# Start addresses of the large tiles in a two-layer graph network: three fill tiles

## The chip, the cores and the metric

The kernel runs on one core of a Trainium2 chip. The metric is the device time of one execution in microseconds; the number before is the median of three runs. A profiled execution supplies the trace that the views below are taken from. PE is the tensor engine, DVE the vector engine, ACT the scalar engine, POOL is GpSimd, and SP issues most of the loads.

## The reference

`x` is 8 batches of 2,048 nodes with 64 features (fp32), `adj` a 2,048 x 2,048 matrix in which the nonzero values of a row are all 1 / (their number). Two layers, each with a layer norm over `x + layer(x)`:

```python
# layer 0: per-node weights from an embedding of 16 numbers
w = einsum('nd,dkio->nkio', embedding, weight)
b = einsum('nd,do->no', embedding, bias)
As = [I, adj, 2 * adj @ adj - I]
x_g = einsum('knm,bmc->bnkc', stack(As), x)
x = layernorm(x + einsum('bnki,nkio->bno', x_g, w) + b)
# layer 1: [x, A x, 2 A A x - x] twice (both supports are adj), then one projection
x = layernorm(x + concat(x0, A x0, 2 A A x0 - x0, A x0, 2 A A x0 - x0) @ W1 + b1)
```

## The kernel before

The product of `adj` with node features is called a hop. There are four of them (two for each layer), each over 16 blocks of 128 source nodes. For each block a slab of `adj` is loaded into a tile `raw` (lines 170 to 175, or 506 in the last stage), and DVE turns it into a tile `s` of ones and zeros in fp32r (`places` at L179, `places_equal` at L185, `places_counted` at L192). The features of the block are split into two fp32r halves in a tile `hl` of 4,096 bytes in each partition: a rounded copy by ACT (L198) and the remainder by DVE (L199). PE then multiplies, 16 matmuls with 512 columns of the moving operand for each slab of 1,024 nodes. The degree of the node is multiplied in as the sums leave PSUM.

The stages follow one another on PE:

- `hop_x` (first hop, two halves of the target nodes): `add_block`, L206. `s` gives the weights, a half of `hl` is the moving operand. 512 matmuls.
- `hop_z1` (second hop): L388, the other way round. `hl` gives the weights, and `s` is the moving operand. 512 matmuls.
- the mixing with per-node weights, one tile of 128 nodes after another: L314 in `mix0`, plain fp32, 64 rows in each of two row groups, 256 columns; weights from `xt`, `t1` and `z2`, the moving operand is `w`. DVE sums up at L320, and `project` (L333) prepares the second layer.
- the third hop, `hop_h`, in pieces of 4, 8 and 4 target tiles: L206 again, 512 matmuls.
- the fourth hop, first `hop_g` for eight target tiles at once, then `hop_tile` for the others one by one: L206, 512 matmuls, with the `hl` tiles of all 16 blocks kept in the pool `flate`. Layer norm and stores are done beside the matmuls.

`run` (L211) calls the operands of a step two steps ahead of its matmuls. Loads go through SP in program order. `raw` has 6 buffers, `s` has 4, and `hl` has 3 until the fourth hop.

Where the tiles lie: pools take memory from the left or, with `side="right"`, from the right end, one behind the other; each tile is rounded up to 32 bytes in the partition. A tile lies at the same place in all partitions. On the left, 16,384 bytes for descriptors and four constants of 32 bytes each come first, then `flag` (L819) and the pools in the order of lines 63 to 75, `flate` taking the place of `fconst` and `fwork2` later. In the program before, the tiles start as follows (bytes in the partition, and the remainder by 128):

```
flag   16512   0      acc   82784  96      rrow   143584  96
z1     16544  32      eT/xc 94432  96      w0     157408  96
z2     49312  32      raw  102624  96      xt     170720  96
rcol   82080  32      s    127200  96      t1     175392  32
equal  82144  96      hl   143584  96 (flate, fourth hop)
sums   82528  96      z0   184288  96      hl     217056  96 (right)
```

Further buffers of a tile follow at multiples of its size. Rows of `hl` and slices of `s` that a matmul takes start 512 bytes, or a multiple of that, behind the start of their tile.

The lines that the change touches are those of the pools on the right (L70 to L72), the tiles of `keep` (L93 to L98, with `sums` at L485) and `flag`.

Of the kernel before, what the change touches and what calls it, by code (L numbers as in the profile page):

```python
# [8 lines left out]
F32 = mybir.dt.float32  # L9
F32R = mybir.dt.float32r  # L10
I32 = mybir.dt.int32
# [5 lines left out]
P = 128  # L17
# [5 lines left out]
FIRST = 8  # L23
HL = 3
RAW = 6
SLOTS = 3


# [7 lines left out]
def pattern(  # L36
# [23 lines left out]
    def pool(stack, name, bufs, **kw):  # L60
        return stack.enter_context(tc.tile_pool(name=name, bufs=bufs, **kw))

    keep = pool(ctx, "fkeep", 1)
    work = pool(ctx, "fwork", 2)
    xcpool = pool(ctx, "fxc", 4)
    rawp = pool(ctx, "fraw", RAW)
    spool = pool(ctx, "fs", 4)
    psum = pool(ctx, "fps", 4, space=PSUM)

    hops = ctx.enter_context(ExitStack())  # L70
    hpool = pool(hops, "fhl", HL, side="right")
    z0pool = pool(hops, "fz0", 1, side="right")  # L72
    layer0 = ctx.enter_context(ExitStack())
# [22 lines left out]
    nonzero = keep.tile([P, 3 * NT], F32, tag="nonzero", name="nonzero")  # L96
    eps = keep.tile([P, 1], F32, tag="eps", name="eps")
    part = keep.tile([P, B], F32, tag="part", name="part")  # L98
    rrow = const.tile([P, N], F32, tag="rrow", name="rrow")
    ident = const.tile([P, P], F32, tag="ident", name="ident")  # L100
    emb_sb = const.tile([P, NT, D], F32, tag="emb", name="emb_sb")
# [441 lines left out]
def general(  # L543
# [17 lines left out]
    work = ctx.enter_context(tc.tile_pool(name="work", bufs=2))  # L561
    apool = ctx.enter_context(tc.tile_pool(name="adj", bufs=SLOTS))
    ps_hop = ctx.enter_context(tc.tile_pool(name="ps_hop", bufs=2, space=PSUM))
# [59 lines left out]
    def load_block(t, tag):  # L623
        a = apool.tile([P, NT, P], F32, tag="a", name=f"a{t}_{tag}")
        nc.sync.dma_start(out=a, in_=rows(adj, t))
        blocks[t] = a

    def prefetch(o, i, tag):
        if i + SLOTS < NT:
            load_block(o[i + SLOTS], tag)  # L630

    def next_order(o):

        return o[NT - SLOTS :] + o[: NT - SLOTS]

# [119 lines left out]
    with tc.tile_pool(name="slab", bufs=1) as spool:  # L755
        slabs = []
        for k in range(NT):
            nc.scalar.dma_start(out=z[k][:, 0], in_=x[k])
            slabs.append(spool.tile([P, FIRST, P], F32, tag=f"s{k}", name=f"s{k}"))
            nc.sync.dma_start(out=slabs[k], in_=adj[0, k].rearrange("m (t n) -> m t n", n=P))  # L760
        for i in range(SLOTS):
            load_block(FIRST + i, 0)
# [53 lines left out]
def gnn_kernel(tc, x, xT, adj, diag, emb, embT, w0, b0, w1, b1, out):  # L816
    nc = tc.nc
    with tc.tile_pool(name="flag", bufs=1) as fpool:
        flag = fpool.tile([1, 1], I32, tag="flag", name="flag")  # L819
        odd = pattern(tc, x, xT, adj, diag, emb, embT, w0, b0, w1, b1, out, flag)  # L820
        with tc.If(odd > 0):
            general(tc, x, adj, emb, embT, w0, b0, w1, b1, out)
# [39 lines left out]
```

## Time and profile before

| | |
|---|---|
| median of three runs | 861.15 us (861.08 to 861.74) |
| time of the profiled execution | 861.28 us |
| its span, first to last instruction | 859.5 us |
| mean granted clock of PE | 0.995 |
| L206, hops by `add_block`, matmul busy (1,280 + 256) | 293.7 + 58.5 us |
| L388, second hop, matmul busy (512) | 116.3 us |
| L314, mixing, matmul busy (three groups of 1,024, overlapping) | 161.0, 160.0, 159.9 us |
| L320, sums of the mixing on DVE (512) | 246.3 us |

A line of groups gives engine, operation, the tiles written and read, shapes and count, then busy time, the mean ns of one, and the idle time of the engine before them with what ended it. Matmuls are pipelined: the mean of one is its latency, and several are under way at once, so that a pace is to be read from busy time and count or from the starts in the timeline. Each fp32 matmul of the mixing appears as two MATMUL records. [...]

### The profile page before, as it was taken

The page shows a single profiled execution, that of the slowest core. Times are in us where ns is not written, and L with a number is a line of the kernel's source. Part 1 is how long each engine was busy: PE and PEld are TensorE (multiplying, and loading weights), DVE is VectorE, ACT ScalarE, POOL GpSimd, SP SyncE. Part 2 cuts the span into 40 slices and gives each one's busy share as a digit, 9 for nine tenths or more (in the row PEclk, how much of TensorE's full clock was granted, in tenths as well). Part 3 has the DMA queues.
Part 4 walks back from the last instruction along what each step waited for, and adds up shares of the span by engine and source line. Part 5 has one row for each costly group of instructions (what it writes and reads, how often), then busy time and mean ns, then how long its engine had stood idle before and what let it go on. Part 6 is the DMA issues. An engine that isn't in the chain of part 4 may idle for free.

```text
span 859.5 us, 14028 instructions
## 1 busy us (share of the span) xinstructions
PE 834.9 (97%) x5666; PEld 744.9 (87%) x5666; DVE 558.8 (65%) x1146; ACT 162.6 (19%) x311; POOL 118.1 (14%) x125
## 2 busy tenths in 40 slices
PE   7999999999999999999999999999999999999995
PEld 5888888888888999999999999999878888788784
DVE  4336355575467888777787787877866467614562
ACT  2112121121111111111111011111331134201210
POOL 3000000030021222111111111110101020102033
PEclk9999999999999999999999999999999999999998
DMA  9996544444210000000000000000246226641572
GB/s 289 404 220 175 155 133 148 147 144 137 74 37 14 14 13 14 14 13 14 14 13 14 1 14 14 14 13 2 72 156 214 86 85 197 198 146 50 140 215 90
DMA packets 48505, 83.94 MB, mean 98 GB/s; under 512 B 10240, under 2 KB 26624, under 8 KB 48304
## 3 DMA queue, kind: packets, MB, share of 16 engines
q1 hardware_dynamic: 44432, 74.10, 29.0%
q0 software_dynamic: 1408, 4.37, 2.0%
q10 hardware_dynamic: 2592, 4.49, 1.4%
q8 instruction: 47, 0.77, 0.4%
q14 instruction: 26, 0.21, 0.1%
HBM read 78.75 MB, written 4.19 MB: 97 GB/s over the span
## 4 chain that ended last, share of the span: by engine, by line
PE 70%; DVE 17%; issue 7%; POOL 2%; ACT 2%; DMA 1%; DVEq 0%; ACTq 0%; POOLq 0%
PE acc L206 33%; PE pm L314 15%; DVE acc L320 14%; PE accT L388 13%; PE a L206 7%; POOL xc L281 1%; DVE ss L273 1%; ACT sq L272 1%; PE pu L333 1%; POOL xt L414 1%; ACT hl L198 1%; DMA b_sb<-in_b 1%; ACT ln_sd L259 0%; DVE ln_r L261 0%; POOL got L290 0%
## 5 line engine op out<-in xcount | busy, mean ns | idle before, releaser
L206 PE MATMUL acc<-hl,s 128*128 128x512 f32 x1280 | 293.7, 391 | 3.7 <-DVE s L192 2.1
L206 PEld LDWEIGHTS acc<-hl,s 128*128 128x128 f32 x1280 | 240.9, 189 | 55.6 <-issue 3.4
L320 DVE SCALAR_TENSOR_TENSOR acc<-pm,emb_sb,acc 128x256 f32<-128x256 f32 x512 | 246.3, 483 | 47.7 <-PE pm L314 25.1
L314 PE MATMUL pm<-w,xt 64*128 64x256 f32 x1024 | 161.0, 379 | 3.4 <-DVE acc L320 3.4
L314 PE MATMUL pm<-w,t 64*128 64x256 f32 x1024 | 160.0, 376 | 0.2 <-ACT t L242 0.2
L314 PE MATMUL pm<-w,z 64*128 64x256 f32 x1024 | 159.9, 376 | 0.0
L198 ACT CAST hl<-z 128x512 fp32r<-128x512 f32 x128 | 78.1, 622 | 251.9 <-PE acc L206 156.8
L388 PE MATMUL accT<-s,hl 128*128 128x512 f32 x512 | 116.3, 389 | 0.0
L314 PEld LDWEIGHTS pm<-w,xt 64*128 64x128 f32 x1024 | 108.3, 187 | 6.1 <-PE pt L240 3.7
L388 PEld LDWEIGHTS accT<-s,hl 128*128 128x128 f32 x512 | 96.0, 188 | 20.0 <-DVE z L368 0.2
L314 PEld LDWEIGHTS pm<-w,t 64*128 64x128 f32 x1024 | 110.8, 187 | 1.8 <-ACT t L242 0.6
L314 PEld LDWEIGHTS pm<-w,z 64*128 64x128 f32 x1024 | 110.8, 187 | 1.2
L179 DVE TENSOR_SCALAR s<-raw 128x1024 fp32r<-128x1024 f32 x64 | 47.8, 748 | 87.6 <-PE acc L206 77.1
L199 DVE TENSOR_TENSOR hl<-z,hl 128x512 fp32r<-128x512 f32 x128 | 94.5, 746 | 8.1 <-ACT hl L198 8.0
L185 DVE SCALAR_TENSOR_TENSOR s<-raw,rrow 128x1024 fp32r<-128x1024 f32 x32 | 41.3, 1290 | 49.3 <-PE accT L388 43.4
L192 DVE TENSOR_SCALAR_CACHE_REDUCE s<-raw 128x512 fp32r<-128x512 f32 (+1 forms) x48 | 41.2, 860 | 37.5 <-PE acc L206 30.5
L206 PE MATMUL a<-hl,s 128*128 128x512 f32 x256 | 58.5, 389 | 0.9 <-DVE flag L474 0.9
L206 PEld LDWEIGHTS a<-hl,s 128*128 128x128 f32 x256 | 48.0, 188 | 11.0 <-issue 1.0
L414 POOL DMA_DIRECT2D xt<-in_xT x16 | 9.2, 578 | 272.6 <-PE pm L314 201.5
L242 ACT COPY hT<-pt 128x512 f32<-128x512 f32 x16 | 9.4, 586 | 166.5 <-PE pt L240 166.5
L230 POOL TENSOR_TENSOR z<-z,got 128x512 f32<-128x512 f32 x12 | 17.4, 1481 | 160.2 <-ACT got L229 160.1
L340 ACT COPY z<-pu 128x256 f32<-128x256 f32 x64 | 20.7, 375 | 83.5 <-PE pu L333 83.5
(74 smaller groups left out, 339.3 us busy)
## 6 DMA issues: line engine op xcount, KB each, us to landing
raw<-in_adj SPq DMA_DIRECT2D x112, 512.0 KB, 4.3
raw<-in_adj SPq DMA_DIRECT2D x32, 256.0 KB, 2.8
z<-in_x SPq DMA_DIRECT2D x16, 256.0 KB, 8.9
xt<-in_xT POOLq DMA_DIRECT2D x16, 256.0 KB, 2.9
out<-got ACTq DMA_DIRECT2D x16, 256.0 KB, 2.1
w<-in_w SPq DMA_DIRECT2D x6, 256.0 KB, 9.3
rrow<-in_diag SPq DMA_DIRECT2D x1, 1024.0 KB, 8.7
eT<-in_embT ACTq DMA_DIRECT2D x1, 256.0 KB, 3.9
```

Source lines behind the costliest of these rows:

```text
L179: nc.vector.tensor_scalar(s, raw, 0.0, None, ALU.not_equal)
L185: nc.vector.scalar_tensor_tensor(s, raw, 0.0, rrow[:, n0 : n0 + raw.shape[1]], ALU.add, ALU.is_equal, accum_out=count)
L192: nc.vector.tensor_scalar(s, raw, 0.0, 0.0, ALU.not_equal, ALU.add, accum_out=count)
L198: nc.scalar.copy(hl[:, 0], src)
L199: nc.vector.tensor_tensor(hl[:, 1], src, hl[:, 0], ALU.subtract)
L206: nc.tensor.matmul(a, lhsT=s[:, i * P : (i + 1) * P], rhs=hl[:, h], start=(first and h == 0), stop=(last and h == 1),)
L230: nc.gpsimd.tensor_tensor(z[s][t], z[s][t], got, ALU.add)
L314: nc.tensor.matmul(pm[:, j, i], lhsT=tt[k][q, 2 * g + i, :], rhs=w[k][q, ds, :], start=(k == 0), stop=(k == 2),)
L320: nc.vector.scalar_tensor_tensor(part, pm[:, :, :, d, :].rearrange("p j i c -> p (j i) c"), emb_sb[:, t, dd : dd + 1], part, ALU.mult, ALU.add
L340: nc.scalar.copy(bc(s, t)[:, bs, :].rearrange("p (i j) c -> p j i c", j=2), got[:, :, :, 2 - s, :])
L388: nc.tensor.matmul(accs[i][:, c], lhsT=hl[:, h, i * P : (i + 1) * P], rhs=s[:, c * 512 : (c + 1) * 512], start=(k == 0 and h == 0), stop=( ...
L414: nc.gpsimd.dma_start(out=xt, in_=xT[t])
```

## The change

Two tiles that nobody writes or reads are put in (`fill_r` with 96 bytes in the partition at the right end, `fill` with 64 bytes at the end of those of `keep` that are made at the start), and `flag` takes 128 bytes instead of 4, of which the first 4 are used. No instruction is added, removed or moved in the order of the program. By the sizes above, the left side then moves by 96 bytes behind `flag` and by 160 behind `keep`, and the right side by 96 towards the left: `z1` starts at 16,640, `raw` at 102,784, `s` at 127,360, `hl` at 216,960 and, in the fourth hop, at 143,744, all multiples of 128. `t1` and `hT`, which lie behind the small tile `mean`, start at 64 past such a multiple.

```diff
+LINE = 128
...
     hops = ctx.enter_context(ExitStack())
+    pool(hops, "ffill", 1, side="right").tile([P, 24], F32, tag="fill_r", name="fill_r")
     hpool = pool(hops, "fhl", HL, side="right")
...
     part = keep.tile([P, B], F32, tag="part", name="part")
+    keep.tile([P, 16], F32, tag="fill", name="fill")
     rrow = const.tile([P, N], F32, tag="rrow", name="rrow")
...
-        flag = fpool.tile([1, 1], I32, tag="flag", name="flag")
+        flag = fpool.tile([1, LINE // 4], I32, tag="flag", name="flag")[:, 0:1]
```

## The prediction

> **What bounds the kernel now.** I read the page's first part (busy time by engine), its fourth (the chain that ended last), then the groups, then the timeline of PE in four stretches, since the change adds no instruction and can only alter how long existing ones take.
>
> ```profile
> PE 834.9 (97%) x5666; PEld 744.9 (87%) x5666; DVE 558.8 (65%) x1146; ACT 162.6 (19%) x311; POOL 118.1 (14%) x125
> ...
> PE 70%; DVE 17%; issue 7%; POOL 2%; ACT 2%; DMA 1%; DVEq 0%; ACTq 0%; POOLq 0%
> ...
> L206 PE MATMUL acc<-hl,s 128*128 128x512 f32 x1280 | 293.7, 391 | 3.7 <-DVE s L192 2.1
> ...
> L388 PE MATMUL accT<-s,hl 128*128 128x512 f32 x512 | 116.3, 389 | 0.0
> ...
> L388 PEld LDWEIGHTS accT<-s,hl 128*128 128x128 f32 x512 | 96.0, 188 | 20.0 <-DVE z L368 0.2
> L314 PEld LDWEIGHTS pm<-w,t 64*128 64x128 f32 x1024 | 110.8, 187 | 1.8 <-ACT t L242 0.6
> ```
>
> PE works in 834.9 of 859.5 us. The 391 and 389 ns are latencies of overlapping matmuls, so the pace must come from busy time over count: L388 has 116.3 / 512 = 227.1 ns. PE sat idle 0.0 us before that group, so nothing outside PE makes its pace. The timeline gives it without the edges (columns: start us, length us, engine, line, count):
>
> ```profile
> 9.32 2.33 PE L206 MATMUL acc<-hl,s 128*128 128x512 f32 x5
> ```
> ```profile
> 41.83 24.42 PE L206 MATMUL acc<-hl,s 128*128 128x512 f32 x107
> ```
> ```profile
> 126.15 116.25 PE L388 MATMUL accT<-s,hl 128*128 128x512 f32 x512
> ```
> ```profile
> 300.14 0.63 PE L314 MATMUL pm<-w,t 64*128 64x256 f32 x4
> 300.57 0.63 PE L314 MATMUL pm<-w,z 64*128 64x256 f32 x4
> 301.01 0.63 PE L314 MATMUL pm<-w,xt 64*128 64x256 f32 x4
> ```
>
> Taking off the last matmul's own 0.63 us (slow clock) or 0.39 us: (2.33 - 0.63) / 4 = 426 ns at the start; (24.42 - 0.39) / 106 = 226.7 ns in hop_x; (116.25 - 0.39) / 511 = 226.7 ns in hop_z1; in the mixing stage four matmuls per 0.43 us, and over all of its undisturbed pairs 215.8 ns a pair. Now the columns. 426.7 ns for 512 columns is 1.2 columns per ns, without remainder. At double that clock 512 columns would take 213.3 ns; the trace shows 226.7. So the excess of 13.3 ns is there only at full clock, and 226.7 / 213.3 = 17/16. In the mixing stage the pair, which also changes weights for each matmul, is within 2.5 ns of 213.3.
>
> **Why 17/16.** One fp32r row of the moving operand (hl at L206, s at L388) is 512 x 4 = 2,048 bytes in each partition: 16 lines of 128 bytes when it starts on a line, and it starts at 96 past one, so it touches 17. If the operand is fetched by whole lines and a line takes 213.3 / 16 = 13.3 ns, 17 lines take 226.7 ns. Lines of 64 bytes would give 33/32, 220.0 ns; of 256 bytes 9/8, 240.0 ns. At the slow clock the array needs 426.7 ns, longer than 17 lines, and the excess vanishes, as seen. L314 moves 256 columns in about 216 ns, so a row of 9 lines (120 ns at that rate, if fetched once) would hide. This is an inference from four paces; no operand of 2,048 bytes in this trace starts on a line, so the trace can't show the other case.
>
> **What the Trainium skill says.** "TensorE: Matmul & The Clock Gate", section Back-to-back issue gap, gives N / 1.2 ns cold and N / 2.4 + 2.5 ns warm: 426.7 and 215.8 at N = 512. The trace agrees cold (426.7) and for the mixing pair (215.8), and differs by 10.8 ns in the fp32r hops. "SBUF — State Buffer", section Specifications (TRN2), names lines of 16 bytes: every tile here starts at a multiple of 32, so by that page the change would do nothing; its section Operand start alignment says that its own runs on alignment timed nothing. "DMA: Bandwidth & Descriptors", section How a descriptor splits into AXI transactions, counts in 256 bytes: raw rows start at 224 past such a multiple before and at 128 past it after (102,624 + 160), still off, so I take no gain for the loads.
>
> **The change part by part.**
> - Instructions: none added or removed; the fills are never written. The addresses on the left move by 96 (flag) and, behind keep, by 160; on the right by -96. The hl of hop_x and of the third hops (1,024 matmuls) become aligned by fill_r; the s of hop_z1 (512) and the late hl (512) by flag and fill. t1 and hT, behind mean, go from 32 to 64 past a line: not aligned, but they are weights of fp32 matmuls or ScalarE outputs.
> - Overlaps: the late hl tiles lie over constants, z0 and so on. Both sides shift by fixed amounts, and by the addresses each late hl lies over the same tiles as before: no new wait.
> - f32r pace: 1,976 of the 2,048 hop matmuls (1,536 at L206, 512 at L388) follow the one before within 229 ns; the others are cold (8) or stand behind a wait. Cost of an aligned one, bounded: not above 226.7 unless rival 4 holds, not below 213.3 (512 columns at full clock). I take 215.8, which this trace shows as PE's own pace and the skill gives for 512 columns. Gain 10.83 ns x 1,976 = 21.4 us; at the lower bound 13.33 x 1,976 = 26.3 us.
> - Is it all on the path? The chain runs through L206 and L388 in one piece each, and cover is there: a step of 16 matmuls becomes 3.45 us instead of 3.63.
>
> ```profile
> 50.19 0.69 DVE L179 TENSOR_SCALAR s<-raw 128x1024 fp32r<-128x1024 f32 x1 [2.28 <-PE acc L206]
> 50.84 0.69 DVE L199 TENSOR_TENSOR hl<-z,hl 128x512 fp32r<-128x512 f32 x1
> ```
> ```profile
> 627.56 0.69 DVE L192 TENSOR_SCALAR_CACHE_REDUCE s<-raw 128x512 fp32r<-128x512 f32 x1 [0.47 <-PE acc L206]
> ```
>
> DVE waits 2.28 us of each such step for PE, and 0.47 us in the short steps of the third hops (8 matmuls, 1.81 us becoming 1.73): 2.10 and 0.38 are left. A step loads 512 KB, 152 GB/s at the new pace; the page shows up to 404 GB/s. So PE stays the bound there. If DVE's cover of 0.38 us were gone, its excess would be paid 32 times.
> - Waits that stay: the start (8.3 us), two gaps of 2.5 and 1.9 us between hops where PE waits for s, the tail after the last matmul (10 us).
> - Mixing (242 to about 609 us, L314): within 2.5 ns of its columns, no gain. DVE, ACT and POOL: an operand shorter by one line might gain up to one line's 13 ns; at L320 (483 ns) that would lie beside PE, so nothing.
>
> Sum against the profiled execution: span 859.5 - 21.4 = 838.1; its time 861.28 (1.8 us around the span) becomes 839.9. The median of the runs, 861.15, is 0.1 lower: 839.7.
>
> **Rivals.**
> 1. The forecast: lines of 128 bytes, 839.7. Own range 833.5 (at 213.3 ns, and some of the delayed matmuls gain as well) to 844 (a fifth of the gain lost in waits).
> 2. The 13.3 ns are a fixed cost of fp32r, of its weights' change for instance. For: weights are loaded before each matmul, 188 ns, and both forms of alignment in the trace (96 for all moving operands) look alike, so nothing separates them. Against: the mixing stage changes weights as often, with 187 ns loads, at 215.8 ns; and a fixed number of PE cycles would show at the slow clock. It gives 861.15, no change; so does a fill that takes no space because nothing uses it.
> 3. Lines are real, but a second limit stands close behind, the weight load (188 ns and then 39 ns to the next matmul) or the feeding of s. Any pace between 215.8 and 226.7; in the middle 221.2 ns, 1,976 x 5.4 = 10.7 us, 850.4. Its range is 844 to 858. Against: 188 ns loads keep a pace of 216 ns in the mixing stage, in another row grouping.
> 4. Slower: operands at the same place of their lines get in each other's way. Now z2 as weights (32 past a line) and w (96) differ; afterwards both are at 0. In the trace xt, at 96 like w, has matmuls of 379 ns against 376 for t and z at 32: 3 ns on z's 1,024 matmuls is 3.1 us, 864.2. It decides where the hops gain under 1.5 ns each. Against: s and hl are both at 96 already, so their relation stays, and 379 may come from waits, which L314's xt group has (3.4 us).
>
> **How the numbers follow.** Forecast 0.70, rival 3 0.12, rival 2 0.11, rival 4 0.07. Range 833.5 to 858 holds rivals 1 and 3, 0.82 less their edges. 0.2% (1.7 us) is what can be told from no change: faster 0.82, same 0.11, slower 0.07.
>
> **What would show it.** Right: the one piece of 512 matmuls at L388 shrinks from 116.25 to about 110.9 us, L206 by as much per matmul, L314's groups and LDWEIGHTS at 188 and 187 ns stay, the slow-clock pace stays 426.7, busy PE is near 813. Wrong: a pace of 226.7 in spite of aligned hl and s (rival 2), one in between (3), longer L314 (4), or new idle time of PE before L206 of more than a few us.

## The result, and the profile after

The changed kernel takes 861.66 us in the median of four runs; the kernel before, in four runs beside it, takes 861.30: a ratio of 1.0006 with a 95% interval of 0.9989 to 1.0023. In a second, longer series (below) it was 1.0001, 0.9992 to 1.0011. The change made no difference; 839.7 us had been forecast.

The profiled execution was the longest of the four, 863.26 us with a span of 861.4. The page of the changed kernel (lines are numbered three higher) shows the three groups that the forecast rested on:

```profile
L209 PE MATMUL acc<-hl,s 128*128 128x512 f32 x1280 | 296.2, 394 | 3.7 <-DVE s L195 2.1
...
L317 PE MATMUL pm<-w,z 64*128 64x256 f32 x1024 | 159.8, 376 | 0.0
...
L391 PE MATMUL accT<-s,hl 128*128 128x512 f32 x512 | 116.3, 389 | 0.0
L391 PEld LDWEIGHTS accT<-s,hl 128*128 128x128 f32 x512 | 96.0, 188 | 20.1 <-DVE z L371 0.2
```

L391 is busy for 116.3 us as before, to the last digit; 110.9 had been forecast. The mixing at L317 stayed too (159.8 us for `z`). The timeline of PE, with the columns as before, gives the pace in the first hop and at the slow clock:

```profile
9.08 2.33 PE L209 MATMUL acc<-hl,s 128*128 128x512 f32 x5
```
```profile
41.64 24.64 PE L209 MATMUL acc<-hl,s 128*128 128x512 f32 x108
```

(24.64 - 0.39) / 107 = 226.6 ns for each matmul, and (2.33 - 0.63) / 4 = 425 ns at the slow clock: what the kernel before had. The aligned row of 16 whole lines is no faster than the row that touched 17.

The 2.5 us that L209 is longer are no effect of the places. From one matmul's start to the next, 18 intervals at that line take 426 or 427 ns, against 6 before: five more at the start, where the pace changed to 227 ns 1.9 us later, and seven in a spell of 3.4 us at half clock behind a gap in the third hop. The windows view has it, first before and then after the change (the granted clock is the third number from the right):

```profile
636.00:650.00 14.00, 11.87 (x52) 1.00 0.47 137
```
```profile
636.00:650.00 14.00, 11.87 (x50) 0.88 0.38 111
```

Twelve intervals of 200 ns extra are 2.4 us. Such a spell, which costs half of its length, about 1.7 us by this estimate, stands in the traces of eight experiments below as well (256 columns, 64 weight columns, bf16 unaligned, the three offsets of `hl`, and `hl` lower by 64 and by 128). So the experiments with one run are compared by their paces rather than by their times.

The loads look better at first sight: the median from issue to landing of the weights `w` fell from 9.3 to 6.3 us. That is scatter: the same kernel in a later execution (the last experiment below) has 8.3 us. Here are the lines of the two executions, from the DMA part of their pages:

```profile
w<-in_w SPq DMA_DIRECT2D x6, 256.0 KB, 6.3
```
```profile
w<-in_w SPq DMA_DIRECT2D x6, 256.0 KB, 8.3
```

### The profile page after: what moved, and what is told of

Its sections match the earlier page's. It is cut to its first block, busy times and chain, and to the rows that moved or that the text cites. A ratio compares the mean times of both kernels' runs of the same rounds, so it can differ in the third digit from the quotient of the medians.

```text
span 861.4 us, 14028 instructions
## 1 busy us (share of the span) xinstructions
PE 837.4 (97%) x5666; PEld 746.6 (87%) x5666; DVE 559.0 (65%) x1146; ACT 162.6 (19%) x311; POOL 118.2 (14%) x125
## 4 chain that ended last, share of the span: by engine, by line
PE 81%; DVE 9%; issue 4%; ACT 2%; POOL 1%; DMA 1%; DVEq 0%; ACTq 0%; POOLq 0%
PE acc L209 33%; PE pm L317 26%; PE accT L391 13%; DVE acc L323 8%; PE a L209 7%; PE pu L336 2%; POOL xc L284 1%; ACT hl L201 1%; DMA b_sb<-in_b 1%; ACT sq L275 1%; PE pt L243 1%; DVE ss L276 0%; POOL xt L417 0%; DMA raw<-in_adj 0%; POOL got L293 0%
## 5 line engine op out<-in xcount | busy, mean ns | idle before, releaser
L209 PE MATMUL acc<-hl,s 128*128 128x512 f32 x1280 | 296.2, 394 | 3.7 <-DVE s L195 2.1
L209 PEld LDWEIGHTS acc<-hl,s 128*128 128x128 f32 x1280 | 242.7, 190 | 56.1 <-issue 3.2
L317 PE MATMUL pm<-w,xt 64*128 64x256 f32 x1024 | 161.0, 379 | 3.3 <-DVE acc L323 2.2
L317 PE MATMUL pm<-w,t 64*128 64x256 f32 x1024 | 159.9, 376 | 0.2 <-ACT t L245 0.2
L317 PE MATMUL pm<-w,z 64*128 64x256 f32 x1024 | 159.8, 376 | 0.0
L391 PE MATMUL accT<-s,hl 128*128 128x512 f32 x512 | 116.3, 389 | 0.0
L317 PEld LDWEIGHTS pm<-w,xt 64*128 64x128 f32 x1024 | 108.3, 187 | 6.0 <-PE pt L243 3.6
L391 PEld LDWEIGHTS accT<-s,hl 128*128 128x128 f32 x512 | 96.0, 188 | 20.1 <-DVE z L371 0.2
L317 PEld LDWEIGHTS pm<-w,t 64*128 64x128 f32 x1024 | 110.7, 187 | 1.8 <-ACT t L245 0.6
L317 PEld LDWEIGHTS pm<-w,z 64*128 64x128 f32 x1024 | 110.8, 187 | 1.3
L202 DVE TENSOR_TENSOR hl<-z,hl 128x512 fp32r<-128x512 f32 x128 | 94.4, 745 | 10.8 <-ACT hl L201 10.7
L209 PE MATMUL a<-hl,s 128*128 128x512 f32 x256 | 58.4, 389 | 0.9 <-DVE flag L477 0.9
L209 PEld LDWEIGHTS a<-hl,s 128*128 128x128 f32 x256 | 48.0, 188 | 10.9 <-issue 1.0
```

Of the source, the lines that this page charges most:

```text
L202: nc.vector.tensor_tensor(hl[:, 1], src, hl[:, 0], ALU.subtract)
L209: nc.tensor.matmul(a, lhsT=s[:, i * P : (i + 1) * P], rhs=hl[:, h], start=(first and h == 0), stop=(last and h == 1),)
L317: nc.tensor.matmul(pm[:, j, i], lhsT=tt[k][q, 2 * g + i, :], rhs=w[k][q, ds, :], start=(k == 0), stop=(k == 2),)
L391: nc.tensor.matmul(accs[i][:, c], lhsT=hl[:, h, i * P : (i + 1) * P], rhs=s[:, c * 512 : (c + 1) * 512], start=(k == 0 and h == 0), stop=( ...
```

## The experiments

Edits are to the changed kernel unless stated. "Pace" is the time from one matmul's start to the next in an undisturbed stretch. It is worked out from a line of the timeline as above, or as the mean of all such intervals of a stage.

### Is the excess a fixed cost, the weights, or a slower rate?

256 columns at a time in the second hop:

```diff
-                    for c in range(2):
+                    n = 512 if k in (0, NT - 1) else 256
+                    for c in range(HALF // n):
                         nc.tensor.matmul(
-                            accs[i][:, c], ..., rhs=s[:, c * 512 : (c + 1) * 512],
+                            accs[i]...[:, c * n : (c + 1) * n], ..., rhs=s[:, c * n : (c + 1) * n],
```

> The changed kernel, but 14 of every 16 steps of the second hop (L391 there) move 256 columns at a time: 64 matmuls of 512 columns and 896 of 256, with the weights loaded before each. The line theory of the prediction is refuted by the aligned kernel, which still has 226.7 ns for 512 columns. Theory A, a fixed cost per fp32r matmul: 106.7 + 13.3 = 120.0 ns for each of 256 columns, the kernel 896 x 120.0 - 448 x 226.7 = 6.0 us longer. Theory B, the weight load sets the pace (128 columns of 4 bytes take 226.7 ns whatever is moved): the pace stays near 226.7 ns for 256 columns, the kernel about 101 us longer. Theory C, the columns themselves run at 16/17 of the clock: 113.3 ns, no change in time.

```profile
134.86 43.36 PE L392 MATMUL accT<-s,hl 128*128 128x256 f32 x360
```
```profile
L392 PE MATMUL accT<-s,hl 128*128 128x256 f32 x896 | 107.8, 283 | 0.0
```

These are the timeline and the group of this kernel: (43.36 - 0.28) / 359 = 120.0 ns. It took 869.17 us, 7.8 more than the kernel before (861.34 beside it), where theory A had 6.0 and the spell accounts for 1.7. 120.0 is 106.7 + 13.3: the excess is the same for half the columns, so theory C falls, and the weight load (192 ns for one in this hop, with more than one under way) doesn't set the pace, so B falls in that form.

Fewer weight columns, 64 and in a later run 32:

```diff
+                        m = P if k in (0, NT - 1) else P // 2
-                            accs[i][:, c], lhsT=hl[:, h, i * P : (i + 1) * P], ...
+                            accs[i][:m, c], lhsT=hl[:, h, i * P : i * P + m], ...
```

> The changed kernel, but 14 of every 16 steps of the second hop take 64 instead of 128 weight columns; half of the sums of these steps is left out. 512 columns are moved as before. Theory B (weight load): a load of half the size ends earlier, the pace falls from 226.7 ns to PE's own, 213 to 216 ns, so 448 x 11 to 13 ns = 5 to 6 us less. Theories A (fixed cost) and C (slower columns): 226.7 ns stay, no change in time.

> As the run with 64 weight columns (229.7 ns, between 224 and 236), with 32: three quarters of the sums of 14 of 16 steps of the second hop are left out. If the fixed part is the time that the weights' bytes take from the moving operand: 213.3 + 13.3 / 4 = 217 to 219 ns. If it is fixed: 226.7 ns or more.

The groups of the kernel with 64 columns, and the timeline of the one with 32:

```profile
L392 PE MATMUL accT<-s,hl 128*64 128x512 f32 x448 | 103.4, 392 | 0.0
L392 PEld LDWEIGHTS accT<-s,hl 128*64 128x64 f32 x448 | 60.1, 134 | 42.8
```
```profile
139.67 30.51 PE L392 MATMUL accT<-s,hl 128*32 128x512 f32 x131
```

The times are 864.39 and 863.02 us. With 64 columns the intervals repeat 224, 227, 234, 230, 236, 229 ns, a mean of 229.7 in the hop; with 32 columns the mean is 231.2. One weight load falls to 134 and 109 ns. Shorter loads didn't shorten the pace here, they made it uneven and longer, which none of the theories had; that the fixed part is the time of the weights' bytes is refuted. Why they lengthen it wasn't settled.

64 rows at a time, in pairs of row groups:

```diff
-            for i in range(B // 2):
+            for r in (0, 2):
+                for i in range(2):
...
+                            for j in range(2):
+                                q = slice(j * C, (j + 1) * C)
-                            accs[i][:, c], lhsT=hl[:, h, i * P : (i + 1) * P], ...
+                                accs[i + 2 * j][:, c], lhsT=hl[q, h, (i + r) * P : (i + r + 1) * P], rhs=s[q, ...],
```

> The changed kernel with the second hop's fp32r matmuls cut to 64 rows, two at a time in the two row groups and in different banks, as the mixing does in fp32 (1,024 matmuls of 512 columns in 512 pairs at L391). The two halves of a sum are not added up and two blocks' products fall on one sum, so this hop's values are left out of the result. If the fixed 13.3 ns belong to weights of 128 rows: 215.8 ns a pair, 110.5 us for the hop and 5.6 us less in all. If they belong to fp32r in any shape: 226.7 ns a pair, 116 us, no change.

```profile
139.80 30.55 PE L394 MATMUL accT<-s,hl 64*128 64x512 f32 x268
```

For 134 pairs that is (30.55 - 0.39 - 0.02) / 133 = 226.6 ns a pair, where 0.02 us is how much later the second of a pair starts. Over the whole hop, 951 of 1,022 intervals from one pair to the next take 226 or 227 ns. The others stand mostly at the beginnings of the hop's two halves, up to 1.0 us long, and make the hop 119.7 us instead of 116.3; what PE waited for there was not followed up. The kernel took 866.57 us. The pair in plain fp32 (mixing) takes 215.8. So the 13.3 ns go with fp32r, not with 128 rows, and the prediction's argument against rival 2, that the mixing keeps 215.8 ns, says nothing about fp32r.

bf16 for `s` and both halves:

```diff
-F32R = mybir.dt.float32r
+F32R = mybir.dt.bfloat16
```

> The changed kernel with s and both halves of hl in bf16 instead of fp32r in all four hops: ones and zeros stay exact, the remainder of the split carries fewer bits. 2,048 matmuls of 512 columns with weights loaded before each. Theory A in the form of a cost of every change of weights with 128 rows, of any type: 226.7 ns, no change. Theories B and C, which rest on 4 bytes per element: 213 to 216 ns, 21 to 27 us less than the changed kernel (about 835 to 841 us), if nothing else takes over.

The first hop and the second in the timeline of this kernel:

```profile
41.81 24.55 PE L209 MATMUL acc<-hl,s 128*128 128x512 bf16 x113
```
```profile
139.66 30.60 PE L391 MATMUL accT<-s,hl 128*128 128x512 bf16 x141
```

(24.55 - 0.38) / 112 = 215.8 ns. The kernel takes 839.34 us, a ratio of 0.9741 (0.9725 to 0.9758) to the kernel before. What the prediction expected of aligned operands, bf16 gives, and the rest of the sum held: 22.0 us against the kernel before, where the sum had 21.4. The gain has a price in digits of the remainder.

### Do the places of the tiles matter at all?

The kernel before, unaligned, with the same line for bf16:

> The kernel before, whose tiles start at 32 or 96 past a multiple of 128, with s and hl in bf16 instead of fp32r (remainders with fewer bits). If starts at multiples of 32 bytes are all alike to PE: 215.8 ns as in the aligned bf16 kernel and about 839.3 us. If bf16, without the fixed cost that fp32r has, lays a cost of lines open that fp32r hid: more than 215.8 ns, up to 17 or 9 lines for 16 or 8, so 228 to 240 ns.

The first hop of this kernel:

```profile
41.81 24.55 PE L206 MATMUL acc<-hl,s 128*128 128x512 bf16 x113
```

839.55 us in one run and 215.8 ns in both hops: alike. Then `hl` off the multiples of 32:

```diff
-        hl = pool.tile([P, 2, B * C], F32R, tag=tag, name="hl")
+        hl = pool.tile([P, 2 * B * C + 8], F32R, tag=tag, name="hl")
+        hl = hl[:, 1 : 1 + 2 * B * C].rearrange("p (h c) -> p h c", h=2)
```

with 1 element (4 bytes), 4 (16 bytes) and 2 (8 bytes), and as a control with 0:

> The changed kernel, but every hl tile is 32 bytes longer and its data begin 4 bytes past a multiple of 32, so the moving operand of L209 and the weights of L391 are off 8, 16, 32, 64 and 128 bytes alike, and ACT and DVE write there. If PE fetches without regard to lines of any of these sizes: 226.7 ns, 188 ns for a weight load, no change. If lines of 16 bytes matter (one more than 128 of them): up to 228.4 ns at L209, 3 us more; of 32 bytes 65/64, 230.2 ns, 5 us more; more than that if each column straddles.

> As the 4-byte offset of hl, but 16 bytes past a multiple of 32 (the 4-byte offset cost 10.8 ns for each matmul at L209 and 5.2 ns at L391, against the aligned kernel). If PE reads in lines of 16 bytes or less: 226.7 ns in both hops, about 861.5 us. If in lines of 32 bytes: slower than 226.7 ns at L209, near the 237.5 ns of the 4-byte offset, about 880 us.

> As before, 8 bytes past a multiple of 32. If the grain is 8 bytes or less: 226.7 ns. If it is 16 bytes: between 226.7 and 237.5 ns at L209, or the same 237.5 ns where any straddled line costs the same. If 32 bytes: like the 16-byte offset.

> Control for the three offsets: hl tiles are 32 bytes longer as there, but their data begin at the start of the tile. The hl tiles then start at 32, 64 and 96 past a multiple of 128 in turn (in the fourth hop at 0, 32, 64, 96). If the offsets inside 32 bytes are what cost: 226.7 ns at L210 and L392, about 861.5 us. If the other size or the other places of the tiles cost: 230 ns or more, 870 us or more, and the offsets prove nothing.

| data of hl begin at | time, us | first hop, ns | second hop, ns |
|---|---|---|---|
| 4 bytes into the tile | 882.93 | 238.0 | 232.0 |
| 8 bytes | 876.55 | 234.9 | 231.7 |
| 16 bytes | 874.72 | 233.8 | 230.3 |
| 0 bytes (control) | 873.00 | 233.5 | 231.6 |

The timeline of the first hop with 4 bytes, and of the control:

```profile
41.71 24.70 PE L210 MATMUL acc<-hl,s 128*128 128x512 f32 x103
```
```profile
41.73 24.44 PE L210 MATMUL acc<-hl,s 128*128 128x512 f32 x104
```

(The expectation for 16 bytes took the excess of the first as 10.8 ns; by all intervals of the hop it is 11.3.) The control overturned the first reading. With whole multiples of 32 and no offset, the longer tile alone costs 11.4 us against the kernel before. Against the control, the offsets add 4.5, 1.4 and 0.3 ns in the first hop; in the second, 16 bytes even take off 1.3.

What the longer tile changes are the places of its copies: 4,128 bytes apart, they stand 32, 64 and 96 bytes past `s` modulo 128. In the fourth hop the 16 tiles lie in the order in which they are used, each 32 bytes further from `s` than the one before, and the mean pace of the 16 matmuls of each step forms a table (moving operand's start minus that of the weights):

```
bytes apart        0     32     64     96    128    160    192    224
steps 1 to 8     227   233.6  229.4  233.1  233.3  234.1  232.6  232.8   ns
bytes apart      256    288    320    352    384    416    448    480
steps 9 to 16  227.0  233.6  229.4  233.1  233.2  234.1  232.7  232.7   ns
```

(The first step starts with a gap; 227 is its later matmuls.) The second row repeats the first, so for these differences the pace goes by their value modulo 256, and of the eight values only 0 gives 227.

Two things limit this rule. First, an offset of `hl` changes the difference too, so the offsets are no pure test of where a tile starts. With 4 bytes the steps of the fourth hop past the first take 234.8 to 239.9 ns, all above the 234.1 of the control. With 16 bytes, the fourth and the eighth step of each row (differences of 112 and 240 modulo 256) have 226.6 or 226.7 ns again, while the first hop, where by the addresses one of the three tiles has the difference 240 as well, has no step of that pace. Off the multiples of 32 the difference modulo 256 doesn't settle the pace, and what does stays open. Second, where the control's fourth hop goes on tile by tile, `hl` changes after every second matmul; the mean there is 232.4 ns, and the tiles with difference 0 have intervals of 226 to 236 ns, apart from one behind a gap. The rule was seen where the difference stays the same over many matmuls.

The next four runs move `hl` of the first three hops alone:

```diff
-    pool(hops, "ffill", 1, side="right").tile([P, 24], F32, tag="fill_r", name="fill_r")
+    pool(hops, "ffill", 1, side="right").tile([P, 32], F32, tag="fill_r", name="fill_r")
```

(32, 40, 56 and 88 elements for 32, 64, 128 and 256 bytes more.) Their expectations took the steps in the order of the node blocks instead of the order of use, and so expected a relation modulo 512:

> The changed kernel with fill_r 32 bytes longer: in the first three hops hl lies 32 bytes lower against s than in the changed kernel; in the fourth it is unchanged. If the relation of moving operand and weights counts: about 232.9 ns in hops one to three (as in the steps of the control's fourth hop whose hl has this place in 512 bytes), 226.7 ns in the fourth, 1,536 x 6.2 ns = 9.6 us more. If the length of the tile was what cost: 226.7 ns everywhere, no change.

> As before with 64 bytes. Relation counts: about 229.4 ns in hops one to three, 226.7 ns in the fourth, 4.1 us more. Length: no change.

> As before with 128 bytes. Relation modulo 128: 226.7 ns everywhere, no change. Relation modulo 512, as the steps of the control with this place had it: 226.7 ns too. If 227 ns need the two operands at one place in 512 bytes: slower, 229 to 234 ns in hops one to three.

> As before with 256 bytes. Relation modulo 128, or 256: 226.7 ns everywhere, no change, as in the kernel before, where hl and s are 256 apart in 512. Relation in 512 bytes as in the control's steps with this place: 233.2 ns in hops one to three, 10 us more.

| hl lower by | time, us | hops 1 and 3, ns | hop 2, ns | hop 4, ns |
|---|---|---|---|---|
| 32 | 871.34 | 233.3 | 233.3 | 226.7 |
| 64 | 870.43 | 233.3 | 229.0 | 226.7 |
| 128 | 871.35 | 232.4 | 232.4 | 226.7 |
| 256 | 861.00 | 226.7 | 226.8 | 226.7 |

Here are 128 bytes, first and fourth hop:

```profile
41.60 24.80 PE L209 MATMUL acc<-hl,s 128*128 128x512 f32 x106
```
```profile
761.70 19.66 PE L209 MATMUL acc<-hl,s 128*128 128x512 f32 x86
```

and 256 bytes, first hop:

```profile
41.82 24.42 PE L209 MATMUL acc<-hl,s 128*128 128x512 f32 x107
```

In one and the same execution (24.80 - 0.39) / 105 = 232.5 ns stand beside (19.66 - 0.39) / 85 = 226.7, with `hl` 128 bytes off `s` in the first and at its place in the second. 64 bytes even show the sign: in hop 2 the roles are exchanged and the difference is +64 (229.0, in the table 229.4), in hops 1 and 3 it is -64 (192: 233.3, in the table 232.6). Away from 0, then, one difference can give paces up to 1 ns apart in two hops.

Now the change itself can be read. Before, `hl` minus `s` is 217,056 - 127,200 = 89,856 = 351 x 256; after, 216,960 - 127,360 = 89,600 = 350 x 256. The left side went up by 160 and the right down by 96, together exactly 256. The change moved everything and left this relation alone. Half of the change should then cost, so the part on the right was taken out:

```diff
-    pool(hops, "ffill", 1, side="right").tile([P, 24], F32, tag="fill_r", name="fill_r")
```

> The change without its part on the right: the left side moves by 96 and 160 bytes as in the change, hl of hops one to three and z0 stay where they were before, 96 bytes off s in 256. If the relation of the operands counts: 233.1 ns at L208 in hops one and three, 234.1 ns in hop two, 226.7 ns in the fourth, in all 1,024 x 6.4 + 512 x 7.4 = 10.3 us more than before, about 871.6 us. If only starts inside 32 bytes count: no change.

The timeline of this kernel in the first, second and fourth hop:

```profile
41.60 24.66 PE L208 MATMUL acc<-hl,s 128*128 128x512 f32 x105
```
```profile
139.63 30.62 PE L390 MATMUL accT<-s,hl 128*128 128x512 f32 x130
```
```profile
761.80 19.43 PE L208 MATMUL acc<-hl,s 128*128 128x512 f32 x85
```

233.4, 234.3 and 226.7 ns; 872.39 us, a ratio of 1.0125 (1.0104 to 1.0145). The forecast had been 871.6. Here `hl` lies where it lay before the change and `s` has moved; in the four runs above `s` stayed and `hl` moved. Neither tile's own place makes the difference, but the two together.

Whether bf16 is sensitive to the relation (aligned bf16 kernel, `fill_r` with 56 elements):

> The aligned bf16 kernel with fill_r 128 bytes longer, so that hl lies 128 bytes off s in 256 in hops one to three. If the relation counts only where 4 bytes are read for each column: 215.8 ns everywhere, about 839.3 us. If it counts for every type: some ns more in hops one to three, as the 5.8 ns that fp32r paid here.

838.18 us in one run, 215.8 ns in all hops: at 128 bytes it isn't. Last, the changed kernel again in five rounds:

> The changed kernel once more, in more rounds, to narrow the interval around no change. If all starts at multiples of 32 bytes are alike: a ratio of 0.999 to 1.001 to the kernel before. If a small part of the change is worth something (fewer lines for the loads or for DVE), below 0.999.

861.43 us, ratio 1.0001 (0.9992 to 1.0011).

## Why the prediction was wrong

- **What bounds the kernel**: right. PE sets the time in the hops, and a pace of 215.8 ns in all of them makes 839.3 us (the bf16 kernel), where the sum had 839.7. So the number of matmuls, the cover of DVE and the loads, and the waits that stay held, as far as their sum shows it.
- **"Why 17/16"**: the step that failed. From 226.7 / 213.3 = 17/16 the prediction concluded that a row touching 17 lines of 128 bytes takes 17 line times. Rows on 16 whole lines take the same 226.7. The excess is 13.3 ns for each fp32r matmul at full clock, with 256 columns (120.0) as with 512, with 64 rows as with 128; 17/16 came about because 13.3 is a sixteenth of 213.3. The gain of 10.83 ns for each of 1,976 matmuls was therefore nothing. All of its fp32r paces had been taken at 512 columns, so a fixed cost and a proportional one looked alike.
- **Rival 2** (fixed cost, 861.15 us, chance 0.11) is what happened. Both arguments against it were weak: the mixing stage is plain fp32, which with two row groups keeps to 215.8 ns, while fp32r in the same two row groups takes 226.7; and a fixed cost need not be a fixed number of cycles, since at the slow clock it isn't seen at all (426.7). Its suspect, the change of weights, isn't confirmed: fewer weight columns don't lower it. What makes the 13.3 ns stays open. fp32r takes in 512 columns of 4 bytes in 226.7 ns; a record of plain fp32 in the mixing took in 256 columns of 4 bytes in 215.8, bf16 512 columns of 2 bytes in 215.8, and fp32r at the slow clock needs 426.7. So these three take in about half as many bytes in a ns, and none of them shows the excess. That fits a limit in reading operands, but no run tests it.
- **Rival 3** (lines real, a second limit behind them): falls with the lines.
- **Rival 4** (operands in each other's way by their places) had the right pair of suspects with the sign reversed: fp32r was fastest with both operands at one place, and the other multiples of 32 cost. It named z2 and `w` of the mixing, where nothing changed (159.9 and 159.8 us). Its argument that the relation of `s` and `hl` stays was right for the result, but only modulo 128; what counts is 256, and that 160 + 96 meets it is luck: the fills were chosen for 128. The 861.15 us of rival 2 came out because its cost is fixed and because of this luck; without `fill_r` its number would have been 1.25% off.
- **The trace showed one side only**: all large tiles shared the remainder 32 by 64. The prediction said so, and still gave 0.70 to an inference from a ratio.
- **The Trainium skill**: "SBUF — State Buffer", section Specifications (TRN2), with its lines of 16 bytes, had been read to mean that the change does nothing. That came true in the sum, but not for that reason: with every tile still at a multiple of 32, leaving out `fill_r` cost 1.25%. The gap of N / 2.4 + 2.5 ns that "TensorE: Matmul & The Clock Gate", section Back-to-back issue gap, gives for a single matmul is met in the stream of bf16 matmuls here (215.8) and not in that of fp32r (226.7 at best).
- **Loads**: no gain, as costed; a 512 KB slab of `raw` landed after 4.3 us before and 4.0 and 4.1 us after. The reason given, 256-byte transactions, isn't tested by any run: the section that the prediction names there speaks of bytes that are fetched, and `raw` is where the loads write.

## What to carry to other kernels

A ratio of two paces is no mechanism: before an excess is put down to a rate, look for the same instruction at another size, since a fixed and a proportional cost are one number at one size. In a kernel with long streams of fp32r matmuls like these, compare where the moving operand and the weights start, modulo 256 bytes in the partition; the same place was the fastest of the multiples of 32 here. A small tile put in on one side only cost 1.25%, and a shift of both sides hid what each half would have done. When a tile is lengthened to test an offset, run the longer tile without the offset too.

## What the runs showed of the hardware

- An fp32r matmul of 512 columns with its own weights takes 426.7 ns at the slow clock; half of that, 213.3, is 13.3 less than the 226.7 it takes at full clock. With 256 columns it takes 120.0 (106.7 + 13.3). bf16 takes 215.8 for 512.
- In streams where the difference of its operands' starts stays the same, multiples of 32 bytes other than 0 (modulo 256) made an fp32r matmul 2.3 to 7.6 ns slower (229.0 to 234.3). At 0, with `hl` and `s` both at 224 or both at 128 past a multiple of 256, it was 226.7; other places with that difference weren't tried. bf16 shows nothing of it at 128.
- With the moving operand 4 bytes past a multiple of 32, the first hop took 238.0 ns against 233.5 in the control, with 16 bytes 233.8. Whether the start or the difference to the weights does this isn't shown.
